# A two-layer graph kernel on one core: the product h = A·m put in a written order, with its shorter parts moved

## The chip, the cores and the metric

The kernel runs on one core of one Trainium2 chip. The metric is the device time of one execution in microseconds (us). Before the change three runs took 648.65, 652.32 and 649.35 us; their median is 649.35 us.

## What is computed

The inputs are x (2708 × 128) and a 0/1 matrix adj (2708 × 2708). Two layers follow each other, each ended by a layer norm. The change lies in the second layer, after `num`:

```
# layer 0: diffusion over the normalised adj, and attention masked by adj
x  = layernorm(x + L0(x, adj))
# layer 1
XW  = x @ W
Z   = leaky_relu(s_row[:, None] + s_col[None, :], 0.01)
den = exp(Z)
num = adj @ den
att = where(num != 0, den / num, 0)
M   = att @ XW
H   = adj @ M
x   = layernorm(x + H)
```

## The kernel before

The program `grouped` is built for TensorE (PE), VectorE (DVE), ScalarE (ACT), GpSimd (POOL) and the queue that issues loads (SP). Columns of a 2708-wide row are cut in six strips of SW = 512, the last (`TAIL` to N) of 148. Rows are cut in NB = 22 blocks of P = 128. The transposed matrix `adj_t` is read from memory; what the kernel holds is transposed too, so M is gathered as `m_acc` (128 features × 512 nodes for each strip) and then turned back by PE transposes.

**The interval loop (L1530 to L1589).** The second layer's `num` and M are made over NG = 24 groups ("intervals") of nodes, with a lag: in a step PE multiplies group `step` (`num`), ACT and DVE make the quotient of group `step - 1`, and PE weighs group `step - 2` into five accumulators `m_acc` (`weigh`), one for each strip of 512. The 148 columns at the end are kept aside in `tails` and weighed late into a sixth accumulator, `m_tail` (`weigh_tails`): 23 of its 24 products are issued at step NG (L1589), the 24th at L1590.

**M's rows (m_rows, L1519).** For each strip: an accumulator is copied to `mt` (`to_mt`, ACT for even strips and DVE for odd ones), four PE transposes turn it (`rows_of`), DVE scales the result into `m` and splits it into `m_hi` and `m_lo`, two halves of its bits. Strips 0 to 2 are turned inside the last step (`m_rows(s - 2)` at L1559), strips 3 to 5 after it (L1592).

**h (L1625 to L1757).** H transposed is `m`ᵀ·`adj_t`, accumulated over the 22 row blocks, once with `m_hi` and once with `m_lo`. It is made in parts of columns, and each part in loads of `n` row blocks into one of six rooms in SBUF (`h_rooms`: the four `ring` tiles, the first of which is `x_sb`, then `wt` and `xws`), used in turn:

- part one, columns 512 to 1536, two blocks a load: 11 loads of 1 MB, eight products of 512 columns for each;
- part two, columns 1536 to 2048, three blocks a load, and beside it columns 0 to 512 from a copy in bf16 (`a16_d`, named `a_d` in the trace): eight loads of 768 KB + 384 KB (the last has one block), twelve products each;
- part three, columns 2048 to 2560, four blocks a load: six loads (the last has two blocks), eight products each;
- the 148 last columns, from `last_short`, already in SBUF: 44 products of 148 columns (`last_columns`).

I number the loads 0 to 24: part one is 0 to 10, part two 11 to 18, part three 19 to 24. Load i uses room i mod 6. Each load is converted by DVE to `rounded` (3 buffers), and ACT takes the low bits of every word for a check (`low_bits_of`, writes `junk`); a room can be filled again when both are done. In part two POOL also converts the bf16 copy to `short` (2 buffers). The 148 last columns are converted by POOL to `last`.

When a part is finished (`finished`, L1641), ACT copies each accumulator to `ht`; then `stats` (four PE transposes, a DVE addition into `hh`, mean and variance on DVE, the root `rstd` on ACT) and `norm` (reciprocal on DVE, normalising by DVE and POOL, the output transfer on POOL's queue). `hh` has 2 buffers; a third one waits for the transfer out of the first. These steps are put on a list `waiting` and taken one after each load of the next part.

**What sets the order.** Operations through `mm`, `dve`, `act` and `gps` are pinned in the order of the text while the list `strict` is not empty. In the interval loop it is not empty. It is cleared at L1594, so in all of h the scheduler of the framework sets each engine's order; the products of h call `nc.tensor.matmul` itself.

Of the kernel before, what the change touches and what calls it, by code (L numbers as in the profile page):

```python
# [9 lines left out]
F32 = mybir.dt.float32  # L10
# [37 lines left out]
def grouped(  # L48
# [29 lines left out]
    def blocks(s):  # L78
        return min(SW // P, NB - s * (SW // P))
# [149 lines left out]
    def over(t, m, n):  # L229
        return t.unsqueeze(2).to_broadcast([P, m, n])  # L230
# [1200 lines left out]
    tails = flow.tile([P, NG, N - TAIL], F32, name="tails")  # L1431
# [75 lines left out]
    def to_mt(s):  # L1507

        _, i0, i1 = strips_m[s]
        op = ("copy", "tensor_copy")[s % 2]  # L1510
        (dve if s % 2 else act)(op, mt[:, i0:i1], accs[s][:, : i1 - i0])

    def rows_of(t, b0, n):
        rows = ps_num.tile([P, SW // P, P], F32, tag="num", name="rows")
        for b in range(n):
            mm(nc.tensor.transpose, rows[:, b, :], t[:, ts(b, P)], ident)
        return rows

    def m_rows(s):  # L1519

        b0, n = s * 4, blocks(s)
        m = m_p.tile([P, SW // P, D], F32, tag="m", name="m", bufs=2)
        dve(
            "tensor_tensor", m[:, :n, :],
            rows_of(mt[:, b0 * P :], b0, n)[:, :n, :], over(back[:, b0 : b0 + n], n, D),
            ALU.mult,
        )
        halves(m_hi[:, b0 : b0 + n, :], m_lo[:, b0 : b0 + n, :], m[:, :n, :])

    for step in range(NG + LAG):  # L1530
        g, before, first = step, step - 1, step - LAG
        if g < NG:
            qs[g] = flow.tile([P, N], F32, tag="q", name="q", bufs=LAG + 2)
        for s, item in enumerate(strips_m):
# [19 lines left out]
            if first > 0 and s < NS - 1:  # L1554
                weigh(first, *item)
                if first == NG - 1:
                    to_mt(s)
                    if s > 1:
                        m_rows(s - 2)  # L1559
# [27 lines left out]
        if step == NG:  # L1587
            accs.append(ps_num.tile([P, SW], F32, tag="num", name="m_tail"))
            weigh_tails(range(first + 1))  # L1589
    weigh_tails(range(first, NG))  # L1590
    to_mt(NS - 1)
    for s in range(NS - 3, NS):  # L1592
        m_rows(s)
    strict.clear()  # L1594
    main.close()

    strict.append("checks")

    lens = tab.tile([P, 2 * NG], F32, name="lens")
    dve("tensor_copy", lens[:, :NG], k_of)  # L1600
    dve("tensor_copy", lens[:, NG:], j_of)
    lens_ps = ps_num.tile([P, SW], F32, tag="num", name="lens_ps")
    nc.tensor.matmul(lens_ps[:, : 2 * NG], ones, lens, start=True, stop=True)
    no = tab.tile([P, 4], F32, name="no")

    dve("tensor_reduce", no[:, 0:1], lens_ps[:, : 2 * NG], AX.X, ALU.max)
    dve("tensor_scalar", no[:, 0:1], no[:, 0:1], G + 0.5, None, ALU.is_gt)
    dve("tensor_reduce", no[:, 1:2], lens_ps[:, NG : 2 * NG], AX.X, ALU.add)
    dve("tensor_scalar", no[:, 1:2], no[:, 1:2], float(N), None, ALU.not_equal)
    wild = tab.tile([P, 3], F32, name="wild")  # L1610
    for k, src in enumerate((sr_p, sc_p)):
        dve(
            "tensor_reduce",
            wild[:, k : k + 1], src, AX.X, ALU.max, apply_absolute_value=True
        )
    dve("tensor_scalar", wild[:, 2:3], beta_sb, LIMIT / STEEP, None, ALU.mult)
    dve(
            "tensor_reduce",
        no[:, 2:3], wild, AX.X, ALU.max, apply_absolute_value=True
    )  # L1620
    dve("tensor_scalar", no[:, 2:3], no[:, 2:3], LIMIT, None, ALU.is_gt)
    strict.clear()
# [3 lines left out]
    k = 0  # L1626
# [7 lines left out]
    last = hp.tile([P, NB * (N - TAIL)], F32R, name="last")  # L1634
# [6 lines left out]
    def finished(done, final=False):  # L1641

        short = done[0][1] < SW
        ht = (
            hp.tile([P, 2 * P], F32, name="ht_short") if short else
            turn.tile([P, NB * P], F32, tag="t", name="ht")
        )
        steps = []
        for i, (acc, w_, ib) in enumerate(done):
            nb = (w_ + P - 1) // P  # L1650
            mine = ht[:, i * SW : i * SW + nb * P]
            if w_ < nb * P:
                nc.gpsimd.memset(mine[:, w_:], 0.0)
            nc.scalar.copy(mine[:, :w_], acc[:, :w_])
            hh = hp.tile([P, 4, D], F32, tag="hh", name="hh", bufs=2)
            got = []

            def stats(ib=ib, nb=nb, hh=hh, got=got, mine=mine):
                rows = rows_of(mine, 0, nb)
                nc.vector.tensor_tensor(  # L1660
                    hh[:, :nb, :], rows[:, :nb, :], x1[:, ib : ib + nb, :], ALU.add
                )
                got.extend(moments(hh, nb))

            def norm(ib=ib, nb=nb, hh=hh, got=got):
                mv, rstd = got
                dve("reciprocal", rstd[:, :nb], rstd[:, :nb])
                for b in range(nb):
                    (dve if final or b % 2 else gps)(
                        "tensor_scalar", hh[:, b, :], hh[:, b, :], mv[:, b, 0:1],  # L1670
                        rstd[:, b : b + 1], ALU.subtract, ALU.mult,
                    )
                full = min(nb, N // P - ib)
                q = nc.scalar if final else nc.gpsimd
                q.dma_start(
                    out[ib * P : (ib + full) * P, :].rearrange("(b p) d -> p b d", p=P),
                    hh[:, :full, :],
                )
                if full < nb:
                    q.dma_start(out[(ib + full) * P : N, :], hh[:LAST, full, :])  # L1680

            steps += [stats, norm]
        return steps

    waiting = []

    def products(kb, ways):
        for part, m in enumerate((m_hi, m_lo)):
            for acc, rows in ways:
                nc.tensor.matmul(  # L1690
                    acc[:, : rows.shape[-1]], m[:, kb, :], rows,
                    start=(kb, part) == (0, 0), stop=(kb, part) == (NB - 1, 1),
                )
# [4 lines left out]
    def part(p0, p1, n, short=False):  # L1698

        nonlocal k  # L1700
        w_ = p1 - p0
        accs_h = [bank() for _ in range(p0, p1, SW)]
        acc_short = bank() if short else None
        for kb in range(0, NB, n):
            m = min(n, NB - kb)
            room = h_rooms[k % len(h_rooms)]
            k += 1
            a = room[:, : m * w_]
            nc.sync.dma_start(
                a.rearrange("p (b i) -> p b i", b=m), rows_at(kb, m, p0, p1)  # L1710
            )
            t = widened(a, "rounded", 2048, dve, 3)
            low_bits_of(a, hp.tile([P, 2048], I16, tag="junk", name="junk", bufs=1))
            if short:
                a = room.bitcast(BF16)[:, 2 * n * w_ :][:, : m * SW]
                nc.sync.dma_start(a, a16_d[:, kb * SW : (kb + m) * SW])
                ts_ = widened(a, "short", n * SW, gps, 2)
            for b in range(m):
                ways = [
                    (acc, t[:, b * w_ + i * SW : b * w_ + i * SW + SW])  # L1720
                    for i, acc in enumerate(accs_h)
                ]
                if short:
                    ways.append((acc_short, ts_[:, ts(b, SW)]))
                products(kb + b, ways)
            if waiting and kb > 0:
                waiting.pop(0)()
        done = [(acc, SW, p0 // P + 4 * i) for i, acc in enumerate(accs_h)]
        return done + ([(acc_short, SW, 0)] if short else [])

    def last_columns():

        w_ = N - TAIL
        flat = last_short.rearrange("p b i -> p (b i)")
        for b in range(2):
            c = ts(b, NB // 2 * w_)
            gps("tensor_copy", last[:, c], flat[:, c])
        acc = bank()
        for kb in range(NB):
            products(kb, [(acc, last[:, ts(kb, w_)])])  # L1740
        return [(acc, w_, TAIL // P)]

    waiting += finished(part(SW, 3 * SW, 2))
    waiting += finished(last_columns())
    waiting += finished(part(3 * SW, TAIL - SW, 3, short=True))
    done = part(TAIL - SW, TAIL, 4)
    while waiting:
        waiting.pop(0)()
# [4 lines left out]
    nc.tensor.matmul(no_ps[:, 0:1], ones, wild[:, 1:2], start=True, stop=True)  # L1753
    odd = late.tile([P, 1], mybir.dt.int32, name="odd")
    dve("tensor_scalar", odd, no_ps[:, 0:1], 0.5, None, ALU.is_gt)
    for step in finished(done, final=True):
        step()  # L1757
# [437 lines left out]
```

## Time and profile before

| | us |
|---|---|
| median of three runs | 649.35 |
| the profiled execution | 652.04 |
| span of that execution | 649.3 |
| PE busy in the span | 608.8 |
| DVE, ACT, POOL busy in the span | 491.4, 471.3, 289.2 |

All times below are from the start of the span. The interval loop ends its last `num` product at about 557; the first product of h starts at 576.02 and the last at 638.99; the last transfer out is issued at 644.54. A "group" line names the line of the kernel, the engine, the operation, what it writes and reads, and the count. Where one helper line (L198, L207, L212, L217, L222) stands for many operations, go by the tile names. A matmul in the timeline has a duration in the pipeline; what it costs is the distance to the start of the next. A square bracket tells how long the engine had been idle before, and what ended it.

### The profile page before, as it was taken

The page shows a single profiled execution, that of the slowest core. Times are in us where ns is not written, and L with a number is a line of the kernel's source. Part 1 is how long each engine was busy: PE and PEld are TensorE (multiplying, and loading weights), DVE is VectorE, ACT ScalarE, POOL GpSimd, SP SyncE. Part 2 cuts the span into 40 slices and gives each one's busy share as a digit, 9 for nine tenths or more (in the row PEclk, how much of TensorE's full clock was granted, in tenths as well). Part 3 has the DMA queues.
Part 4 walks back from the last instruction along what each step waited for, and adds up shares of the span by engine and source line. Part 5 has one row for each costly group of instructions (what it writes and reads, how often), then busy time and mean ns, then how long its engine had stood idle before and what let it go on. Part 6 is the DMA issues. An engine that isn't in the chain of part 4 may idle for free.

```text
span 649.3 us, 8555 instructions
## 1 busy us (share of the span) xinstructions
PE 608.8 (94%) x2859; PEld 351.9 (54%) x2859; DVE 491.4 (76%) x978; ACT 471.3 (73%) x649; POOL 289.2 (45%) x270
## 2 busy tenths in 40 slices
PE   7999999999999899998878899999999999989993
PEld 4445345465655676765664344444444444658872
DVE  5765865764699756756885999899999999599575
ACT  4767786767889521410585999999999999778652
POOL 6967778777798742000123322333232230021573
PEclk9999999999999899999988999999999999999997
DMA  8968989988971999989956999756689453259981
GB/s 270 392 221 330 317 301 363 360 329 310 335 262 70 276 390 389 387 267 375 394 205 185 238 223 246 214 168 175 193 217 267 170 170 129 87 202 383 390 320 53
DMA packets 66407, 171.64 MB, mean 264 GB/s; under 512 B 10059, under 2 KB 19285, under 8 KB 63333
## 3 DMA queue, kind: packets, MB, share of 16 engines
q1 hardware_dynamic: 42500, 107.01, 46.4%
q0 software_dynamic: 22464, 62.25, 34.5%
q10 hardware_dynamic: 1392, 1.77, 0.8%
q8 instruction: 24, 0.39, 0.2%
q14 instruction: 27, 0.21, 0.1%
HBM read 171.89 MB, written 5.72 MB: 274 GB/s over the span
## 4 chain that ended last, share of the span: by engine, by line
PE 65%; ACT 13%; DVE 10%; POOL 6%; issue 4%; DMA 1%; another core or an unknown queue 0%; DVEq 0%; POOLq 0%; ACTq 0%
PE num L198 11%; PE m_acc L198 11%; PE att_acc L207 9%; PE h_acc L1690 7%; PE sim L207 7%; PE dif_acc L207 6%; ACT q L198 5%; POOL total L222 4%; ACT L198 2%; DVE q L198 2%; PE tot L198 2%; PE dif_acc L198 1%; PE sim L198 1%; POOL ss L198 1%; ACT xn L198 1%
## 5 line engine op out<-in xcount | busy, mean ns | idle before, releaser
L198 PE MATMUL m_acc<-q,xws 128*128 128x512 f32 x240 | 121.6, 592 | 0.0
L198 PE MATMUL num<-ring,wt 128*128 128x512 f32 x216 | 98.2, 546 | 3.6 <-DVE q L198 2.2
L222 POOL TENSOR_TENSOR total<-total,p_t 128x512 f32<-128x512 f32 (+1 forms) x67 | 91.8, 1370 | 21.0 <-ACT p_t L217 18.4
L207 PE MATMUL att_acc<-p_t,x_sb 128*128 128x512 f32 x184 | 91.1, 602 | 1.1 <-ACT p_t L217 1.1
L212 DVE SCALAR_TENSOR_TENSOR p_t<-sim,gentle,pieces 128x512 f32<-128x512 f32 x89 | 65.0, 746 | 34.8 <-PE sim L207 25.7
L198 DVE SCALAR_TENSOR_TENSOR q<-sr_b,nc_s,q 128x1536 f32<-128x1536 f32 (+1 forms) x48 | 77.8, 1623 | 17.3 <-ACT q L198 17.3
L217 ACT ACTIVATE p_t<-p_t,shift 128x512 f32<-128x512 f32 (+1 forms) x89 | 64.7, 745 | 33.8 <-DVE p_t L212 31.5
L198 DVE COPY q<-num 128x512 f32<-128x512 f32 (+1 forms) x142 | 83.5, 611 | 4.5 <-PE num L198 4.5
L198 PEld LDWEIGHTS m_acc<-q,xws 128*128 128x128 f32 x240 | 45.3, 190 | 55.0 <-issue 54.8
L198 ACT ACTIVATE q<-q,head,rest 128x1536 f32<-128x1536 f32 (+1 forms) x48 | 70.2, 1508 | 1.6 <-DVE ring L198 1.3
L198 ACT ACT_TABLE_LOAD x52 | 66.7, 1283 | 3.9 <-issue 3.1
L198 PEld LDWEIGHTS num<-ring,wt 128*128 128x128 f32 x216 | 39.0, 190 | 49.1 <-issue 34.2
L198 ACT ACTIVATE q<-q,c_s 128x1536 f32<-128x1536 f32 (+1 forms) x48 | 62.9, 1355 | 0.3
L198 POOL DMA_INDIRECT ring<-in_adj_t,k_no x18 | 20.8, 1154 | 89.1 <-PE num L198 85.6
L207 PEld LDWEIGHTS att_acc<-p_t,x_sb 128*128 128x128 f32 x184 | 31.7, 189 | 35.3 <-ACT p_t L217 18.8
L207 PE MATMUL sim<-xn_t 128*128 128x512 f32 x98 | 47.6, 592 | 0.0
L222 POOL TENSOR_TENSOR x<-x,p_t 128x660 f32<-128x660 f32 (+1 forms) x22 | 35.1, 1596 | 11.3 <-ACT p_t L217 10.6
L198 ACT ACTIVATE row<-row 128x1354 f32<-128x1354 f32 x30 | 39.5, 1318 | 0.3 <-DMA row<-in_adj 0.3
L207 PE MATMUL dif_acc<-strip,x_hi 128*128 128x512 f32 x88 | 37.8, 429 | 0.0
L207 PE MATMUL dif_acc<-strip,x_lo 128*128 128x512 f32 x88 | 36.2, 411 | 0.0
L1690 PE MATMUL h_acc<-rounded,m_hi 128*128 128x512 f32 x88 | 32.4, 407 | 3.7 <-DVE rounded L212 3.7
L198 PE MATMUL num<-x_sb,wt 128*128 128x512 f32 (+1 forms) x72 | 34.4, 570 | 0.7 <-ACT gb L198 0.7
(362 smaller groups left out, 1170.6 us busy)
## 6 DMA issues: line engine op xcount, KB each, us to landing
pieces<-in_adj_t SPq DMA_DIRECT2D x24, 1024.0 KB, 6.8
strip<-in_adj_t POOLq DMA_DIRECT2D x20, 1024.0 KB, 18.3
row<-in_adj SPq DMA_DIRECT2D x30, 677.0 KB, 5.5
nat<-in_adj_t SPq DMA_DIRECT2D x19, 768.0 KB, 7.7
x<-in_adj SPq DMA_DIRECT2D x14, 677.0 KB, 6.2
ring<-in_adj_t SPq DMA_DIRECT2D x9, 1024.0 KB, 5.1
pieces<-in_adj_t SPq DMA_DIRECT2D x7, 512.0 KB, 6.4
x_sb<-in_adj_t SPq DMA_DIRECT2D x4, 768.0 KB, 6.2
```

What stands on the lines that cost most here:

```text
L198: latest[engine] = op(*args, **kwargs)
L207: op(*args, **kwargs)
L212: return getattr(nc.vector, op)(*args, **kwargs)
L217: return getattr(nc.scalar, op)(*args, **kwargs)
L222: return getattr(nc.gpsimd, op)(*args, **kwargs)
L1690: nc.tensor.matmul(acc[:, : rows.shape[-1]], m[:, kb, :], rows, start=(kb, part) == (0, 0), stop=(kb, part) == (NB - 1, 1),)
```

## The change

What is computed stays the same. Seven things change:

1. All of h goes through the pinned helpers and `strict` stays on until the end, so every engine runs h in the order of the text.
2. `weigh_tails` gives 9 products before the last group's five `m_acc` products, and 15 after them.
3. `m_rows`: strip 0 is turned inside the last step, strip 1's transposes stand before the 15 late products, strips 2 to 5 stand between loads 0, 1, 3 and 5 of h. `to_mt` uses DVE for strips 1 and 5 only. `tails` is allocated after the first `q`.
4. Loads are prepared three ahead (`prepare(i + 3)` after the products of load i): transfer, `rounded`, low bits, `short`. The low bits are written into `sr_b` in place of `junk`.
5. When a part ends, its `ht` copies are issued after `prepare(i + 3)`; `stats` and `norm` follow one after each load.
6. The 44 products of the last columns are dealt 11 after each of loads 19 to 22; POOL's two conversions of `last` stand at loads 14 and 16.
7. Load 24's products are made for columns 0 to 255 and then 256 to 511; `ht`, `stats` and `norm` are done for each half, the first normalised by POOL and sent by SP, the second by DVE and sent by ACT. The check on `low_bits` stands between the halves' `stats` and their `norm`.

The diff, cut to its core:

```
+    def m_turned(s):
+        return rows_of(mt[:, s * SW :], 0, blocks(s))
...
-                    if s > 1:
-                        m_rows(s - 2)
+                    if s == 2:
+                        m_rows(0)
...
-            weigh_tails(range(first + 1))
-    weigh_tails(range(first, NG))
-    to_mt(NS - 1)
-    for s in range(NS - 3, NS):
-        m_rows(s)
-    strict.clear()
+            weigh_tails(range(9))
+    turned_m = {1: m_turned(1)}
+    weigh_tails(range(9, NG))
...
+    def prepare(i):
+
+        if i >= len(todo_h):
+            return
+        part, kb = todo_h[i]
...
+        ready[i] = [widened(a, "rounded", 2048, dve, 3)]
+        low_bits_of(a, junk)
+        if part == 1:
+            a = room.bitcast(BF16)[:, 2 * n * w_ :][:, : m * SW]
+            nc.sync.dma_start(a, a16_d[:, kb * SW : (kb + m) * SW])
+            ready[i].append(widened(a, "short", n * SW, gps, 2))
...
+        if i == len(todo_h) - 1:
+            for q in range(2):
+                for b, jb in enumerate(kbs):
+                    for half in range(2):
+                        row = ready[i][0][:, b * SW + q * SW // 2 :][:, : SW // 2]
+                        product(jb, half, h_accs[part][0], row, q * SW // 2)
...
+    prepare(0)
+    last = hp.tile([P, NB * w_last], F32R, name="last")
+    prepare(1)
+    m_rows(1, turned_m[1])
+    to_mt(NS - 1)
+    prepare(2)
+    ends = {len([1 for part, _ in todo_h if part <= k]) - 1: k for k in range(2)}
+    for i in range(len(todo_h)):
+        products(i)
+        if i in (0, 1, 3, 5):
+            s = {0: 2, 1: 3, 3: 4, 5: 5}[i]
+            rows_m = m_turned(s)
+        if i in (14, 16):
+            widen_last(i == 16)
+        prepare(i + 3)
+        if i in (0, 1, 3, 5):
+            m_rows(s, rows_m)
+        if i == 6:
+            copied()
+        if i == 8:
+            no, wild = counts()
+        if steps:
+            steps.pop(0)()
+        if i in ends:
+            ht = room_of_h()
+            for c, acc in enumerate(h_accs[ends[i]]):
+                p0 = 0 if (ends[i], c) == (1, 1) else h_parts[ends[i]][0] + c * SW
+                steps.extend(finished(acc, SW, p0 // P, ht[:, ts(c, SW)]))
+        if i >= len(todo_h) - 6:
+            last_products(11)
+    while steps:
+        steps.pop(0)()
+    ht = room_of_h()
+    ends = [
+        finished(h_accs[2][0][:, q * SW // 2 :], SW // 2, (TAIL - SW) // P + 2 * q,
+                 ht[:, ts(q, SW // 2)])
+        for q in range(2)
+    ]
+    for stats, _ in ends:
+        stats()
     dve("tensor_reduce", wild[:, 0:1], low_bits, AX.X, ALU.max)
     dve("tensor_scalar", no[:, 3:4], wild[:, 0:1], 0.5, None, ALU.is_gt)
     dve("tensor_reduce", wild[:, 1:2], no, AX.X, ALU.add)
...
+    ends[0][1](gps, nc.sync)
+    ends[1][1](dve, nc.scalar)
```

## The prediction

> **What bounds the kernel now.** I first read the stretches (busy time of each engine, granted clock, share of the DMA engines, GB/s), since only the last 90 us change.
>
> ```profile
> core 0: us, PE busy (x) PEld busy (x) DVE busy (x) ACT busy (x) POOL busy (x), PEclk, DMA share, GB/s
> 561.40:576.00 14.60, 12.46 (x75) 9.47 (x73) 7.47 (x9) 8.11 (x10) 2.65 (x2) 1.00 0.22 72
> 576.00:600.00 24.00, 23.16 (x108) 18.36 (x109) 23.32 (x38) 21.60 (x24) 3.25 (x4) 1.00 0.97 356
> 600.00:620.00 20.00, 19.02 (x104) 15.82 (x103) 10.89 (x29) 13.66 (x20) 12.26 (x9) 1.00 1.04 389
> ```
>
> h is made while two things are full at once: PE, and the DMA engines (389 GB/s from 600 to 620). The clock is 1.00, so no term below rests on it. Second, the chain of waits, for what stands between M and h:
>
> ```profile
> 561.56 5.79 PE m_tail L198 x46
> 567.35 2.58 PE m_acc L198 x6
> ...
> 573.55 2.34 issue
> 575.89 1.90 DVE m_hi L198
> 577.79 1.14 DVE rounded L212
> ```
>
> PE weighs 23 tail products (two records each, so 5.79/23 = 0.252 us a product) while ACT's exponential for the last group (562.01 to 564.6) is long done; then h starts at 576.02 and stops until 578.97. Third, the timeline of loads, low bits and POOL:
>
> ```profile
> 565.62 0.37 SPq L1709 DMA_DIRECT2D xws<-in_adj_t  x1
> 576.04 0.37 SPq L1709 DMA_DIRECT2D x_sb<-in_adj_t  x1
> 604.78 1.49 ACT L217 ACTIVATE junk<-ring 128x1536 int16<-128x1536 int16 x1 [1.42 <-DMA ring<-in_adj_t]
> 607.78 1.49 ACT L217 ACTIVATE junk<-ring 128x1536 int16<-128x1536 int16 x1 [1.26 <-DMA ring<-in_adj_t]
> 612.79 1.98 POOL L222 CAST short<-ring 128x1536 fp32r<-128x1536 bf16 x1 [1.27 <-PE h_acc L1690]
> 614.76 2.41 POOL L222 TENSOR_SCALAR hh<-hh,mv,rstd 128x128 f32<-128x128 f32 x2
> 617.47 0.89 POOL L1675 DMA_DIRECT2D out<-hh  x1 [0.30 <-POOL hh L222]
> ```
>
> Load 5 is issued at 565.62, load 6 at 576.04 when its room is free; loads 14 and 15 land at 604.78 and 607.78 (ACT waits for them): three us apart, the pace of a full DMA. PE uses load 14 only at 612.5, eight us later: the last columns' 40 products (599.16 to 603.63, 0.112 us each) gave the loads that lead. Last, the end:
>
> ```profile
> 639.42 0.59 ACT L1654 COPY ht<-h_acc 128x512 f32<-128x512 f32 x1 [0.81 <-PE h_acc L1690]
> 640.81 0.69 DVE L1660 TENSOR_TENSOR hh<-rows,x 128x512 f32<-128x512 f32 x1 [1.11 <-PE rows L207]
> 644.54 0.40 ACTq L1675 DMA_DIRECT2D out<-hh  x1
> ```
>
> Load 24's products begin at 638.18; from there to the end of the span it is 11.1 us, 4.76 of them after the issue of the last transfer.
>
> **The change part by part.** The sum is made against the span of 649.3. (That execution took 652.04 in all; the median of the runs is 649.35, and I move it by the same difference.)
>
> *Start of h.* 9 tail products from 561.56 end at 563.8, when the exponential's first part (562.01 + 1.4) is ready. Then three `m_acc` (2.58), four transposes (0.44), two `m_acc` (1.72), four transposes (0.44), 15 tail products (3.78): 572.8. In the same time DVE scales and splits strip 0 (0.69 + 0.43 + 0.69, from 567) and converts load 0 (1.21) by 570. POOL's two casts of `last` (1.54 and 2.54), beside which DVE's cast of load 0 took 2.57 and `m_hi` 1.90, are gone from here. So h starts at 572.8, 3.2 earlier, and doesn't stop: -6.0 with the idle 2.8 that h has before (577.7 to 578.9, 619.9, 638.2: about 1 each).
>
> *PE without any wait.* One 512-column product costs 0.2335 (the distance between starts). Part one 88 × 0.2335 = 20.55, M's transposes and the count 1.85: 595.2. Part two 20.55 and two sets of transposes 0.95: 616.7. Part three up to load 24: 40 × 0.2335 = 9.34, 44 × 0.112 = 4.93, transposes 1.2: 632.2. So t0, the start of load 24's products, would be 632.2 in place of 638.2.
>
> *The loads.* Load 5's room is `xws`; its first 16 groups are free when the 16th tail product is done. That was at 565.6 and becomes 569.0 + 7 × 0.252 = 570.8. Load 6 needs load 0's low bits: ACT copies strip 4 at about 569.3 and needs 2.1, so 571.4. From 570.8 on the DMA is full; load 5 takes 2.7 (1.05 MB at 390 GB/s) ahead of load 6, so load 6 and all after it come 576.04 - 570.8 - 2.7 = 2.5 earlier than before. PE asks for part two 8.4 earlier (595.2 for 603.6). The lead of eight us falls to about two, and POOL's cast of `short` (1.5 to 2.0) must fit in it: about 0.8 lost at load 11.
>
> *ACT's new order.* The `ht` copies of part one stand behind the low bits of load 13 (10 + 3), and PE's transposes of `ht` stand right after load 11's products. Load 13 lands at 604.78 - 3.0 - 2.5 = 599.3; low bits 1.7, copy 0.6: 601.6. PE is there at 598.8 and waits 2.8. Queued behind: all of loads 12 to 18. After that the loads have their lead again. At the end of part two the same: the copies stand behind the low bits of load 21 (18 + 3). Load 20 landed by 621.2 before (its low bits start then), 21 follows 2.7 later, minus 2.5: 621.4. Low bits 2.1, copy 0.6: 624.1. PE arrives with load 19 done at about 622.1 (595.2 + 0.8 + 21.5 + 2.8 + 1.87), so it waits 2.0. What remains: 32 × 0.2335 + 4.93 + 1.2 = 13.6. So t0 = 637.7, 0.5 earlier than before: the gain of 6.0 is paid back to the loads.
>
> [...]
>
> *The end.* By halves, eight 256-column products of about 0.117. `ht` of the first half is copied beside the second's products; copies 0.37 each, transposes 0.3, additions 0.43 (0.41 for the 256 columns of `ht_short`), 0.7 of mean and variance a half, the check 0.58 (three DVE operations, which lay at 638.13 before, in idle time), reciprocal 0.2, two normalisations by POOL 1.6. If nothing else waits, the second half's addition starts at t0 + 2.8, and SP's transfer is issued 3.7 after that, t0 + 6.5. Before it was 644.54 - 638.18 = 6.4. Halving gains nothing, since POOL (0.79 a block) and the check lie behind it.
>
> But something waits. The second half's `hh` is the buffer of the last columns (two buffers: last, half 0, half 1), and DVE must wait until both transfers of that one have landed. The last columns' transposes come just before t0; addition and statistics 1.2, root 0.35, reciprocal 0.2, POOL 0.9, two issues on POOL 0.3 + 0.63 + 0.57 (630.49 and 631.11), landing 1.6 after the second's issue: released at t0 + 5.5. All of DVE's queue stands behind: the check, both reciprocals, both normalisations. SP's transfer is then issued at t0 + 5.5 + 3.7 = t0 + 9.2 and the span ends 4.76 later: t0 + 13.9. The landing is known only from two rows (1.9 and 1.6); bounds are 1 and 3.
>
> *At nothing:* `sr_b` for `junk` (same write, last read long before), the count's matmul (0.16, in both), the 44 products (same number; but they covered loads before, which is the price above).
>
> Sum: 572.8 for 576.0, waits of 0.8 + 2.8 + 2.0 in place of 2.8, +2.8 at the end: 637.7 + 13.9 = 651.6, +2.3 on 649.3; on the median 651.6.
>
> **The rivals.**
> - *The buffer is free in time* (the last columns' steps run earlier, or the transfers land at once): 637.7 + 11.2 = 648.9. For it: POOL is idle by then. Against: their order fixes them behind load 23's products. Chance 0.15.
> - *The copies don't hold PE:* loads 13 and 21 land three us sooner, so t0 is near 632.2 and the time 632.2 + 13.9 = 646.1, or 643.4 with the first rival. For it: I take the shift of the loads from one issue time. Against: three us between landings is the full DMA. Chance 0.14, at 645.
> - *POOL becomes the bound of part two, slower than before.* From load 15's cast (607.8) its queue holds casts, normalisations, issues and one cast of `last`: with the slow rows 3 × 1.98 + 2 × 2.41 + 2 × 1.78 + 2.54 + 0.62 = 17.5, so load 18 starts at 625.3, for 619.3 in the forecast. 2.0 of it hides in the wait at load 21, 4.0 don't: 655.6; half of the slow rows, 653.6. It decides once POOL is 2 us late at load 18. For it: 1.98 and 2.41 were seen beside DVE's casts. Against: 1.48 and 1.58 too. Chance 0.25.
> - The forecast: 0.46.
>
> **How the numbers follow.** The forecast and the first rival are within 0.5% (3.25 us, about what the runs can tell from no change), save a fifth of the forecast's own spread of 1.5 above. Faster 0.14 (the second rival); slower 0.09 + 0.21 = 0.30; the same 0.56. The range reaches from the second rival's middle to beyond the third's half: 645.5 to 654.5. The likeliest's own range is 649.5 to 653.
>
> **What would show it.** Right: first product of h at 572 to 573.5; PE idle two to four us before the transposes of `ht` after load 11 and about two after load 19, each released by ACT's copy; DVE idle near the end before an addition into `hh`, released by a transfer on POOL's queue. Wrong: no PE idle there, DMA below 370 GB/s between 575 and 625, or POOL's casts releasing PE. If the copies turn out to be ordered elsewhere, or if the rooms refill faster than 2.5 us ahead, the forecast falls.

## The result and the profile after

| | before | after |
|---|---|---|
| median of 20 runs each, us | 650.42 | 655.23 |
| lowest and highest | 648.65, 653.25 | 651.50, 661.80 |
| ratio after to before, 95% interval | | 1.0064 (1.0050 to 1.0078) |
| profiled execution, its span | 652.04, 649.3 | 651.50, 649.7 |

The change made the kernel slower by 0.64%. The forecast was 651.6 with a range up to 654.5, and "the same" as the likeliest; the time lies 0.7 above the range. One run of after (661.80), and below one each of `e5_whole_odd` (661.39) and `e12_halves` (657.42), lie over 1.5% above the fastest of their kernel and are left out of the ratios.

The profiled execution of after is its fastest. It reached the end of the interval loop 4.2 us earlier than the one of before, though up to there the order of work is the same. What made that difference is open; in the profiles of the other edits `m_tail` begins between 558.1 and 560.5. So all marks below are counted from the first row of `m_tail` (561.40 in before, 557.22 in after). Counted so, after is 4.6 longer, about the 4.8 between the medians.

| us after the first row of `m_tail` | before | forecast | after |
|---|---|---|---|
| first product of h | 14.6 | 11.4 | 11.2 |
| low bits of load 14 begin | 43.4 | 40.9 | 39.6 |
| start of load 24's products (t0) | 76.8 | 76.3 | 77.4 |
| issue of the last transfer out | 83.1 | 85.5 | 86.9 |
| end of the span | 87.9 | 90.2 | 92.5 |

Of the 4.6, 0.6 come before t0 and 4.0 after it. First the chain of waits of after (start, us, engine and what it did):

```profile
557.38 2.27 PE m_tail L198 x18
559.65 2.65 PE m_acc L198 x6
564.89 3.78 PE m_tail L198 x30
568.67 1.84 PE h_acc L198 x8
...
613.73 2.01 POOL hh L198
618.63 2.80 PE h_acc L198 x11
```

The tails stand as forecast, 9 and 15, and h follows without the stop it had before. But in part two the chain goes through POOL's normalising. The timeline of after, all engines, shows each wait with what ended it:

```profile
593.84 1.48 ACT L198 ACTIVATE sr_b<-ring 128x1536 int16<-128x1536 int16 x1 [1.43 <-DMA ring<-in_adj_t]
595.32 1.05 ACT L198 COPY ht<-h_acc 128x512 f32<-128x512 f32 x2
595.94 0.66 PE L198 MATMUL rows<-ident,ht 128*128 128x128 f32 x4 [2.54 <-ACT ht L198]
...
605.82 2.34 POOL L198 TENSOR_SCALAR hh<-hh,mv,rstd 128x128 f32<-128x128 f32 x2
608.46 0.88 POOL L1730 DMA_DIRECT2D out<-hh  x1 [0.29 <-POOL hh L198]
609.34 1.49 POOL L198 CAST short<-wt 128x1536 fp32r<-128x1536 bf16 x1
610.88 0.50 PE L198 MATMUL h_acc<-short,m_hi 128*128 128x512 f32 x1 [0.94 <-POOL short L198]
...
613.71 2.82 POOL L198 TENSOR_SCALAR hh<-hh,mv,rstd 128x128 f32<-128x128 f32 x2
616.83 1.12 POOL L1730 DMA_DIRECT2D out<-hh  x1 [0.29 <-POOL hh L198]
617.95 0.62 POOL L198 CAST short<-x_sb 128x512 fp32r<-128x512 bf16 x1
618.63 0.50 PE L198 MATMUL h_acc<-short,m_hi 128*128 128x512 f32 x1 [1.81 <-POOL short L198]
...
638.68 0.58 POOL L1735 DMA_DIRECT2D out<-hh  x1
640.50 0.42 DVE L198 TENSOR_TENSOR hh<-rows,x 128x256 f32<-128x256 f32 x1 [1.68 <-DMA out<-hh]
643.07 0.16 DVE L198 TENSOR_SCALAR odd<-no_ps 128x1 int32<-128x1 f32 x1
644.15 0.38 SPq L1730 DMA_DIRECT2D out<-hh  x1
```

Load 13's data are there at 593.84; ACT takes its low bits first, then copies `ht`, and PE stands for 2.54. Then POOL: behind 2.34 of normalising and 0.88 of an issue its cast for load 16 is late by 0.94, and two loads on the same again by 1.81. At the end DVE waits 1.68 for the transfer of the last columns. The stretches of after around the first wait (columns: busy time of each engine, granted clock of PE, DMA share, GB/s; the last row is two of the slow us alone) show what came on top:

```profile
588.00:593.20 5.20, 5.20 (x24) 3.98 (x22) 2.83 (x11) 3.02 (x4) 2.87 (x2) 1.00 1.04 391
593.20:596.00 2.80, 0.26 (x2) 0.06 (x2) 0.96 (x1) 2.16 (x4) 1.16 (x2) 1.00 1.04 392
596.00:600.00 4.00, 4.00 (x13) 3.24 (x14) 2.95 (x10) 3.23 (x4) 0.37 (x1) 0.59 1.05 391
600.00:604.00 4.00, 4.00 (x21) 3.24 (x20) 3.23 (x6) 2.92 (x4) 2.14 (x2) 0.99 1.04 390
...
598.00:600.00 2.00, 2.00 (x6) 1.57 (x5) 1.83 (x9) 1.72 (x3) 0.00 (x0) 0.50 1.03 390
```

After the idle stretch PE runs at a clock of 0.59 for four us: 13 rows where the next four us have 21. Products start 0.425 apart from 596.7 to 600 and 0.233 before and after. The ten steps from 596.35 to 600.31 took 3.96; with 0.32 for the first, as after the next transposes, and 9 × 0.2335 they would take 2.42: 1.5 lost.

Last, how the span closes. `odd` says whether the check failed; every engine loads it and branches on it over a fallback program that isn't run. By source line, in after: what, count, durations in ns (least, median, most), first and last start:

```profile
L1815 PEldq TENSOR_LOAD <-odd x1: 489/489/489, 643.3 to 643.3; - x1
L1815 SPq TENSOR_LOAD <-odd x1: 486/486/486, 644.6 to 644.6; - x1
...
L2247 PEldq COMPARE_BRANCH  x1: 3917/3917/3917, 643.9 to 643.9; - x1
L2247 PEldq EVENT_SEMAPHORE  x1: 51/51/51, 647.8 to 647.8; - x1
```

And in before:

```profile
L1759 PEldq TENSOR_LOAD <-odd x1: 493/493/493, 640.1 to 640.1; - x1
L1759 ACTq TENSOR_LOAD <-odd x1: 478/478/478, 645.0 to 645.0; - x1
...
L2191 ACTq COMPARE_BRANCH  x1: 54/54/54, 645.5 to 645.5; - x1
L2191 ACTq EVENT_SEMAPHORE  x1: 17/17/17, 648.2 to 648.2; - x1
```

In before `odd` was ready at 639.7, PE had branched long before the end, and only ACT came late: it issued the last transfer, loaded `odd` at 645.0, branched, and its next instruction came 2.7 after that branch. In after `odd` is made last, at 643.07; PE's branch alone takes 3.92 and ends at 647.8, 1.9 before the end. The transfers out end close to that. Their size and the time from issue to landing (us), first the last one of before, then the two of after:

```profile
out<-hh ACTq DMA_DIRECT2D x1, 256.0 KB, 3.0
...
out<-hh ACTq DMA_DIRECT2D x1, 128.0 KB, 1.9
out<-hh SPq DMA_DIRECT2D x1, 128.0 KB, 3.4
```

So of before's 4.76 after the last issue, which I took for a transfer's landing, the landing is 3.0 (at 647.5), and ACT's branch is over 0.7 later. In after SP's transfer lands at 647.6 and PE's branch ends at 647.8: which of the two sets the end there can't be told apart.

### The profile page after: what moved, and what is told of

Its sections match the earlier page's. It is cut to its first block, busy times and chain, and to the rows that moved or that the text cites. A ratio compares the mean times of both kernels' runs of the same rounds, so it can differ in the third digit from the quotient of the medians.

```text
span 649.7 us, 8578 instructions
## 1 busy us (share of the span) xinstructions
PE 607.6 (94%) x2863; PEld 352.6 (54%) x2863; DVE 493.7 (76%) x977; ACT 471.9 (73%) x652; POOL 286.8 (44%) x272
## 3 DMA queue, kind: packets, MB, share of 16 engines
q10 hardware_dynamic: 1136, 1.64, 0.8%
## 4 chain that ended last, share of the span: by engine, by line
PE 70%; DVE 9%; POOL 7%; ACT 6%; issue 4%; DMA 3%; another core or an unknown queue 0%; POOLq 0%; DVEq 0%; ACTq 0%; SPq 0%
PE num L198 16%; PE m_acc L198 16%; PE att_acc L207 9%; PE sim L207 7%; PE dif_acc L207 6%; PE h_acc L198 4%; POOL total L222 4%; DMA ring<-in_adj_t 2%; PE tot L198 2%; DVE rounded L198 1%; PE dif_acc L198 1%; POOL hh L198 1%; PE sim L198 1%; ACT k_ons L198 1%; POOL ss L198 1%
## 5 line engine op out<-in xcount | busy, mean ns | idle before, releaser
L198 POOL DMA_INDIRECT xws<-xw_d,j_no x24 | 27.4, 1142 | 14.4 <-DVE c_s L198 7.4
L198 PE MATMUL num<-x_sb,wt 128*128 128x512 f32 (+1 forms) x72 | 32.8, 546 | 0.7 <-ACT gb L198 0.7
```

What stands on the lines that cost most here:

```text
L198: latest[engine] = op(*args, **kwargs)
```

## The experiments

All are edits of the changed kernel; "with everything mended" is the kernel of `e8_all`. Twelve ran, in three groups, each beside the kernel before (medians 651.01, 650.15, 650.57). t0 and end are counted from `m_tail` in one profile each; PE's waits are those between h's start and t0.

| label | median us | ratio to before, 95% | t0 | end | PE's waits |
|---|---|---|---|---|---|
| after | 655.23 | 1.0050 to 1.0078 | 77.4 | 92.5 | 2.54, 0.94, 1.81 |
| e1_hh3 | 653.31 | 1.0017 to 1.0058 | 77.5 | 90.6 | 2.52, 0.93, 1.81 |
| e2_copies | 649.54 | 0.9966 to 1.0006 | 73.7 | 89.0 | 1.92 |
| e3_whole | 653.65 | 1.0022 to 1.0069 | 77.6 | 92.1 | 2.56, 0.95, 1.81 |
| e4_between | 652.63 | 1.0004 to 1.0053 | 74.8 | 89.2 | 0.72, 0.16, 3.53 |
| e5_whole_odd | 652.40 | 1.0021 to 1.0050 | 78.2 | 91.8 | 2.53, 0.49, 0.90, 1.82 |
| e6_tails | 655.61 | 1.0072 to 1.0132 | 79.0 | 94.2 | 0.49, 2.30, 0.93, 1.81 |
| e7_copies_normdve | 649.89 | 0.9977 to 1.0006 | 72.5 | 88.7 | 0.40, 0.90, 0.33 |
| e8_all | 644.94 | 0.9896 to 0.9941 | 70.1 | 82.5 | 0.17 |
| e9_late | 647.46 | 0.9916 to 0.9962 | 72.6 | 85.1 | 0.36, 0.89, 0.35, 0.22 |
| e10_tails | 645.79 | 0.9900 to 0.9944 | 71.9 | 84.7 | 0.47, 0.17 |
| e11_steps | 644.42 | 0.9882 to 0.9922 | 71.7 | 82.8 | 0.20, 1.37 |
| e12_halves | 647.11 | 0.9916 to 0.9965 | 71.8 | 85.8 | 0.23, 1.45 |

**The buffer at the end.** `e1_hh3`:

```
-        hh = hp.tile([P, 4, D], F32, tag="hh", name="hh", bufs=2)
+        hh = hp.tile([P, 4, D], F32, tag="hh", name="hh", bufs=3)
```

> Edit: hh gets 3 buffers in place of 2, nothing else. Theory (the end waits for the transfer out of the last columns): DVE's addition of the second half no longer waits 1.68 us for the transfer on POOL's queue; it starts right behind the first addition's statistics, all behind it moves by 1.7, so 1.7 us less than the changed kernel's 655.2: 653.5 (653.0 to 654.2). Rival (the wait only hides another one, such as POOL's normalising of the first half or the two issues on POOL's queue): under 0.5 us, 655.0.

653.31. The wait of 1.68 is gone, and the end came 1.9 earlier with all else in place to 0.1. The intervals of the two kernels overlap; the trace carries the verdict: the forecast's wait was real and cost its length.

**The copies of `ht`.** `e2_copies`:

```
         products(i)
+        step = steps.pop(0) if steps else None
+        if i in ends:
+            ht = room_of_h()
...
         prepare(i + 3)
...
-        if i in ends:
-            ht = room_of_h()
...
```

> Edit: at a part's end ACT's copies into ht stand ahead of the preparing of the next load instead of behind it. Theory: PE's idle 2.5 us before the transposes after load 11 is gone, and with it the slow stretch after it (products 0.425 us apart instead of 0.233 from 596.4 to 600.3, granted clock 0.59), some 1.5 us; the two POOL waits (0.9 and 1.8) stay or grow, as POOL's queue is the next to be late: t0 2 to 4 us earlier, 652.2 (651.2 to 653.5). Rival (the loads bound part two: three us from landing to landing): PE only waits at load 13 or 14 for DVE's conversion instead, nothing gained, 655.

649.54, more than either theory gave, and apart from after by its interval; the trace has 3.6 at t0 and 3.5 at the end. The wait of 2.54 is gone. One wait for POOL of 1.92 stands where there were two. And it cost more than its length; the timeline of this kernel:

```profile
608.58 0.50 PE L198 MATMUL h_acc<-short,m_hi 128*128 128x512 f32 x1 [1.92 <-POOL short L198]
608.92 0.54 PE L198 MATMUL h_acc<-rounded,m_lo 128*128 128x512 f32 x1
609.26 0.63 PE L198 MATMUL h_acc<-short,m_lo 128*128 128x512 f32 x1
609.68 0.63 PE L198 MATMUL h_acc<-rounded,m_hi 128*128 128x512 f32 x1
```

Starts are 0.43 apart again, until 612.3: ten steps of 3.98 in place of 2.44, 1.5 lost. The granted clock was 0.63 from 608.5 to 610.5 and 0.52 from 610.5 to 612.5: the slow stretch now stands behind this wait.

**The end in one piece.** `e3_whole` takes the halves back; `e5_whole_odd` moves `odd` in it:

```
-    norm(dve, nc.scalar)
     odd = late.tile([P, 1], mybir.dt.int32, name="odd")
     dve("tensor_scalar", odd, no_ps[:, 0:1], 0.5, None, ALU.is_gt)
+    norm(dve, nc.scalar)
```

> Edit: the last load's products, copy, statistics, normalising (four blocks on DVE) and transfer (ACT's queue) are made for 512 columns at once as in the kernel before, and the check on low_bits stands ahead of the statistics. Theory (the end costs 15.1 us after the start of load 24's products, against 11.1 in the kernel before, and the halves are the cause): back to 11.1 to 11.5, so 3.6 to 4.0 less: 651.4 (650.8 to 652.2). Rival (the end is late because the last columns' steps stand just ahead of it, not because of halves): their statistics and normalising still stand in DVE's and POOL's queues, so only half of it comes back, 653.3.

> Edit: the kernel with the end made for 512 columns at once, and there only the DVE operation that makes the value odd moved from behind the normalising to ahead of it. Theory (the end of the span is set by what follows odd: all engines load the value and branch on it, 6.3 to 6.9 us from odd to the end in the five profiles in which odd stands last): odd is ready 2.2 us or more earlier, and the end goes back to 4.76 us after the issue of the last transfer, as in the kernel before, in place of 6.98: 2.2 less than that kernel's 653.6, 651.4 (650.8 to 652.3). From the start of m_tail to the end of the span 89.9 in place of 92.1. Rival (the last transfer sets the end, and is slow for another reason): nothing, 653.6.

`e3_whole` gained 0.4 in the trace and 0.2% (1.2 us) by the ratio, not 3.6 to 4.0. The rival's 653.3 fits the median (653.65), but the half that it promised is not in the trace. Its ACT issue stands at t0 + 7.5 (6.4 in before), since ACT's root and DVE's statistics of the last columns are still ahead, and from the issue to the end it took 6.98. In `e5_whole_odd` that distance is 6.02, not 4.76, and the times of the two don't differ beyond their intervals. Part of the rest is one latecomer at the close (`e5_whole_odd`, by source line):

```profile
L2231 POOLq EVENT_SEMAPHORE  x4: 17/17/17, 649.2 to 649.9; - x4
L2231 ACTq EVENT_SEMAPHORE  x2: 17/17/17, 649.3 to 651.6; - x2
```

All engines are done by 649.9 but ACT, whose last one comes at 651.6. In `e3_whole` the same is 0.9 late (649.8 and 650.7). Taken off, the distances are 6.1 and 4.3, about as the theory has it; what makes the latecomer is open. In the four kernels below whose end is whole and whose `odd` stands early (`e8_all` to `e11_steps`) the distance is 4.4 to 4.7, with no latecomer.

**The last columns' place.** `e4_between`:

```
-        if i >= len(todo_h) - 6:
-            last_products(11)
+        if i == 10:
+            last_products(2 * NB)
```

with the conversions at loads 5 and 7 in place of 14 and 16.

> Edit: the 44 products of the last columns stand between part one and part two, as in the kernel before, their conversion on POOL at loads 5 and 7; their steps out follow those of part one. Nothing else. Theory (these products cover the loads of part two and POOL's conversions; at the end they hold a buffer of hh): no idle of PE for ht after load 11 and no slow clock (4.0), POOL's two waits down to 1 or less (1.7), no wait for hh at the end (1.7): 648.3 (647 to 650), below the kernel before by what the earlier start of h gives. Rival (the products are as good anywhere, since PE has the same sum of work, and POOL's additional normalising and issues of the last columns now fall in part two): POOL holds PE by as much, 653 to 655.

652.63, neither. No wait after load 11, POOL's down to 0.72. But at the end of part two PE now stands 3.53 for the copies of `ht`, and `hh` is waited for as before (1.87). ACT's low bits of load 19 stood behind the last columns' root, which waited 7.0 for DVE. The timeline of this kernel:

```profile
626.62 0.66 PE L198 MATMUL rows<-ident,ht 128*128 128x128 f32 x4 [3.53 <-ACT ht L198]
627.03 0.48 PE L198 MATMUL h_acc<-rounded,m_hi 128*128 128x512 f32 x1
627.34 0.39 PE L198 MATMUL h_acc<-rounded,m_lo 128*128 128x512 f32 x1
627.57 0.40 PE L198 MATMUL h_acc<-rounded,m_hi 128*128 128x512 f32 x1
```

So the forecast's second wait for `ht` exists; in after POOL had taken its place. After 3.53 of idle the products start 0.23 apart at once, and the granted clock was 1.00 from 626 to 634.

**The start of h.** `e6_tails`:

```
-            weigh_tails(range(9))
+            weigh_tails(range(23))
...
-    weigh_tails(range(9, NG))
+    weigh_tails(range(23, NG))
```

> Edit: in the changed kernel the tail products are given as before, 23 ahead of the last group's m_acc products and one after strip 1's transposes. Nothing else. Theory (the earlier start of h is paid back to the loads and to ACT's order): h starts 3.2 us later, but ht after load 11 is copied no later, so the idle of 2.5 us and the slow clock after it (1.5) go, and the loads come up to 2.5 earlier: the time does not rise, 654.3 (653.0 to 655.7). Rival (the start is a plain gain): 3.2 more, 658.4.

The median (655.61) lies in the theory's range, but what the theory rests on fell. h starts 0.9 later, not 3.2 (the rest of the early start comes from other parts of the change), and the wait for `ht` stays (2.30), since the loads come later too: the first low bits begin 11.2 after `m_tail`, in after 7.8. ACT's copies of `mt` stand ahead of them. The end is 1.7 later in the trace; the intervals of the two kernels' ratios overlap.

**POOL, and all at once.** `e7_copies_normdve` is `e2_copies` with `(by or dve)(` for `(by or (dve if b % 2 else gps))(`. `e8_all` adds `e4_between`'s place and `e5_whole_odd`'s end.

> Edit: the kernel with ACT's copies into ht ahead of the next load, and there all normalising outside the end by DVE, none by POOL (POOL keeps the casts and the issues of the transfers out). Theory (POOL's queue is what holds PE after the copies are mended: short of load 16 is behind 2.30 of normalising and 0.87 of an issue): the idle of 1.9 us before load 16 goes to 0.3 or less, DVE has room for 0.3 us a block: 647.8 (647.0 to 649.0) against 649.5. Rival (the loads are next: they land three us apart): a wait for DVE's conversion or a load of the same length, 649.5.

> Edit: all at once on the changed kernel: copies into ht ahead of the next load, the last columns between part one and part two, normalising by DVE, the end for 512 columns at once with the check ahead of the statistics and odd ahead of the normalising. Theory: PE without any wait from the start of h to the start of load 24's products (70.6 us after the start of m_tail, worked out in the prediction, in place of 77.4), and an end of 11.1 after it as in the kernel before: 81.7 from the start of m_tail in place of 92.5; 644.5 (643.5 to 646.5). Rival (the loads bound part two whatever is done, three us each, so that some of the 6.8 comes back as waits for loads): 647 to 649.

`e7_copies_normdve`: 649.89, the rival. t0 came 1.2 earlier, but 1.63 of waits in three places stand where 1.92 stood in one, and the times don't differ. `e8_all`: 644.94, as the theory. PE runs from h's start to t0 in 58.9 with one wait of 0.17, and the kernel is 0.8% faster than before. The only wait of its timeline there:

```profile
620.98 0.66 PE L198 MATMUL rows<-ident,ht 128*128 128x128 f32 x4 [0.17 <-ACT ht L198]
```

Of the 6.2 between the traces of `e7_copies_normdve` and `e8_all`, 2.4 lie before t0 and 3.8 behind it.

**What each part is worth there.** From `e8_all`, `e9_late` deals the last columns again, `e10_tails` takes the tails back, `e11_steps` adds after `step()`

```
+        if i >= 20 and steps:
+            steps.pop(0)()
```

and `e12_halves` makes that one's end by halves, both normalised by DVE.

> Edit: the kernel with everything mended (644.9), and there only the last columns dealt over loads 19 to 22 again, with their conversion at loads 14 and 16, as the change has it. Theory (these products are the cover of part two's loads): load 11 is asked for 4.9 us earlier, and PE waits for conversions in part two as in the kernel with copies and DVE's normalising alone (0.40, 0.90 and 0.33 us, and the slower products beside them: load 24's start 2.4 later); 85 us from the start of m_tail in place of 82.5, 647.5 (646.5 to 649). Rival (where they stand is the same once copies, POOL and end are mended): 645.

> Edit: the kernel with everything mended, and there the tail products given as before (23, then one). Theory (the earlier start is a plain gain, of h itself 0.9 us and of ACT's low bits and so of the loads 3.3): 1.7 later at the end, as in the same edit on the changed kernel: 646.7 (646.0 to 648.0). Rival (the prediction's: the gain at the start is paid back by waits for loads later, so that nothing is lost when it is undone): 645.

> Edit: the kernel with everything mended, and there two of the waiting steps taken after each load from load 20 on, so that part two's statistics and normalising are done three loads ahead of the end. Theory (in that kernel DVE's four normalisations of part two, 1.12 us at 631.44, and ACT's root ahead of the copy of ht stand in the way of the end, whose last transfer is issued 7.9 us after the start of load 24's products, 6.4 in the kernel before): 1.0 to 1.3 less, 81.3 from the start of m_tail, 643.8 (643.0 to 644.6). Rival (DVE gets the steps at the cost of the conversions of loads 22 to 24, which PE then waits for): 645.

> Edit: the kernel with two steps a load at the end, and there the end by halves again (load 24's products, copies, statistics, normalising on DVE for both halves, transfers by SP and ACT), with the check ahead and odd behind the first half's statistics. Theory (halving gains little even when nothing waits: DVE's fourteen operations on both halves stand behind each other as before, only the first copy, transposes and addition are hidden): 0.0 to 0.4 less than the whole end. Rival (halving is worth the second half of a chain of 3 us): 1.5 less.

`e9_late`: 2.7 later in the trace, as the theory, and its waits are those of `e7_copies_normdve`: the 44 products are the cover of part two. By the ratios it is 1.4, and the intervals overlap. `e10_tails`: 2.2 later in the trace, 0.3 by the ratios, which the intervals can't tell from nothing; the median (645.79) lies between theory and rival, and the start's worth is seen in the trace only. `e11_steps`: its median (644.42) is in the theory's range, but the ratios of the two kernels don't part, and the trace shows the rival: the end after t0 is 11.1 as in before, and PE first waits 1.37 for DVE's conversion of load 24, so the span ends 82.8 after `m_tail`, for 82.5. `e12_halves`: the end is t0 + 14.0 in place of 11.1, and the median 2.7 higher with intervals that do not quite part. The last issue stands 0.5 later (78.9 for 78.4). SP and ACT each issue one and branch after it, the second transfer lands 4.0 after its issue (the single one of `e11_steps` 2.5), and a latecomer of ACT's at the close (643.7, the others 642.3) is in it too. Halving never gained.

## Why the prediction was wrong

- *Start of h:* 11.4 forecast, 11.2 measured. Right in place and size.
- *PE without any wait:* t0 at 632.2, that is 70.8 after `m_tail`. `e8_all` has 70.1. Right.
- *The loads, "2.5 earlier":* mis-sized. Load 14 came 3.7 earlier. ACT's low bits, which free the rooms, began where the forecast had them (7.8 after `m_tail` for 7.9). But the forecast carried the shift of load 6 on to load 14 as if the DMA moved as much in both kernels: it moved 379 GB/s from 578 to 594 in before, 403 from 570 to 590 in after. Over 16 us that makes about 1 of the 1.2 that are missing, an estimate from these two rates. So the 0.8 at load 11 didn't come, and "the gain is paid back to the loads" is wrong as a claim on the start: undoing its part made `e6_tails` slower.
- *ACT's new order:* the wait after load 11 was 2.54 for 2.8, with its cause. The second, 2.0 after load 19, was not there; POOL's 0.94 and 1.81 were, by the third rival's mechanism, and "POOL's casts releasing PE" is what the prediction itself had named as a sign of being wrong. Together they are 2.75, past the 2 us from which that rival was to decide, but less than half of the 6.0 that it put there. Sum of the waits 5.3 for 5.6: right by luck, since 2.75 of it has another cause. It is chance too that this rival's 655.6 lies near the measured time.
- *The step that failed:* "The clock is 1.00, so no term below rests on it." It was read from 561 to 620 in before, where PE's longest idle time was 1.83, just ahead of h's first product; the forecast itself puts 2.8 of idle into PE, and did not ask what the clock does after it. It cost 1.5, the largest single part of the miss in the trace. The products 0.425 apart came with a granted clock of 0.50 (598 to 600 in after), those 0.233 apart with 1.00 (604 to 608). In six of eight profiles with 1.8 or more of idle in h, just one such stretch was followed by slow products, in before and `e4_between` none. By length they don't agree: stretches of 1.82, 1.92, 2.30 and 2.52 to 2.56 were followed by them, 3.53, one of 2.53 and five of 1.81 to 1.83 not. What decides is not shown.
- *The end:* the wait for `hh` was there, 1.68, released at t0 + 5.9 for 5.5, and SP's issue at t0 + 9.6 for 9.2. The last 4.76 were mis-sized: 5.5. Behind that issue lie PE's branch on `odd`, which is made last (to 647.8), and the landing of the second transfer (to 647.6); the two are not separated in this kernel. Together 1.2.
- *The base:* 649.35 was the median of three runs; twenty gave 650.42. That is 1.1 of the 3.6 between 651.6 and 655.2. The trace's part is 2.3: 1.5 clock, 1.2 end, -0.3 waits, -0.2 start. The remaining 0.3 is within the runs.

The direction was held at 0.30 because gains and losses were set against each other. What the forecast lacked is the second price of a wait: the slow products after it, 1.5 in after.

## What to carry over

Where a forecast puts idle time into TensorE, add the slow products that may follow, here about 1.5 us after five of the seven waits of 1.9 us and up, and after one of six of 1.8. With the order fixed by hand, what waits holds all that stands behind it: in after PE stood 2.54 for ACT's copy behind load 13's low bits, and 0.94 and 1.81 for POOL's casts behind its normalising. So a copy that PE waits for belongs ahead of work that waits for a transfer, and work without a load (the 44 products) belongs where loads lead least (dealt out in `e9_late` they cost 2.7 in the trace). And what the program does after its last value, loading it and branching, is part of the end: make that value early (from the last issue to the end of the span it took 6.98 with `odd` last in `e3_whole` and 6.02 with `odd` early in `e5_whole_odd`, 6.1 and 4.3 without the latecomers, and 4.4 to 4.7 in `e8_all` to `e11_steps`; the times of `e3_whole` and `e5_whole_odd` alone do not part).

## What the runs showed of the hardware

- The length of an idle stretch alone did not tell whether slow products followed. In `e5_whole_odd` PE idled 2.53 at the same place as in `e3_whole` (2.56); there products went on 0.23 apart (granted clock 1.00 from 598.8 to 602.0), and it was the later 1.82 that was followed by starts of 0.43. In `e3_whole` it is the other way round: the 2.56 was followed by starts of 0.43 (granted clock 0.71 from 597 to 601), the later 1.81 by 0.23. The timeline of `e5_whole_odd`:

```profile
598.80 0.66 PE L198 MATMUL rows<-ident,ht 128*128 128x128 f32 x4 [2.53 <-ACT ht L198]
599.52 0.39 PE L198 MATMUL h_acc<-short,m_hi 128*128 128x512 f32 x1
599.75 0.39 PE L198 MATMUL h_acc<-rounded,m_lo 128*128 128x512 f32 x1
...
620.52 0.50 PE L198 MATMUL h_acc<-short,m_hi 128*128 128x512 f32 x1 [1.82 <-POOL short L198]
...
621.55 0.62 PE L198 MATMUL h_acc<-rounded,m_lo 128*128 128x512 f32 x1
621.98 0.63 PE L198 MATMUL h_acc<-rounded,m_hi 128*128 128x512 f32 x1
```

- A branch that takes 54 ns by its row is followed by ACT's next instruction only 2.4 to 3.7 us later, and PE's branch takes 3.3 to 4.4; POOL's and SP's next instructions come 0.2 to 0.5 after theirs. What takes that time is not shown.
- DVE's cast of 128×512 for load 18 took 4.52 in after, where the same cast takes 0.41 in `e2_copies`. The timeline of after:

```profile
609.51 4.52 DVE L198 CAST rounded<-x_sb 128x512 fp32r<-128x512 f32 x1 [0.77 <-PE h_acc L198]
610.76 1.56 POOL L198 CAST last<-last_short 128x1628 fp32r<-128x1628 bf16 x1
612.25 1.48 POOL L198 CAST short<-xws 128x1536 fp32r<-128x1536 bf16 x1
```

It ends at 614.03, right behind POOL's three casts in a row (609.34 to 613.73). In `e2_copies` the long one is DVE's cast for load 17, 4.73 where after has 0.96, again beside POOL's three casts (607.05 to 611.42). POOL's pairs of normalisations took 2.34 and 2.82 in part two, 1.61 to 1.64 later.
